# Order of logits, choice and gather in an FFN's token routing, norms on two engines, and output products over all 128 rows

## The chip, the cores and the metric

The kernel runs on one core of a Trainium2 chip. The metric is the time of one execution on the device in microseconds (us). All data are float32, apart from the incidence matrices of layer 1, which the change leaves alone.

## The reference, cut to what matters

Four batches of 128 channels by 64 x 64 tokens (B = 4, C = 128, N = 4096) pass through four layers: a mamba scan (layer 0), a hypergraph convolution with batch norm and SiLU (layer 1), and two blocks of attention and a mixture of experts (layers 2 and 3). Each part of a block works on layer-normed tokens and adds its result to them. The FFN, in short:

```python
# x: layer-normed tokens [B, N, C]; E = 64 experts, K = 8, H = 512
logits = jnp.einsum('bsd,ed->bse', x, gate_w) + gate_b
probs = softmax(logits, axis=1)              # over the tokens
vals, idx = top_k(probs.transpose(0, 2, 1), K)      # 8 tokens for each expert
gathered = ...                               # x at idx: [B, K, E, C]
pooled = jnp.einsum('bked,bke->bed', gathered, vals)
h = gelu(concat(pooled, 1) @ weight1[e], approximate=False)   # per expert
o = concat(h, 1) @ weight2[e]
out = scatter_add(zeros, idx, vals * o)      # back to the 8 tokens of each expert
```

So each expert picks, in each batch, the 8 tokens with the largest softmax over tokens, runs one row through its two matrices, and adds its output to the same 8 tokens with the same weights.

## The kernel before, in words

The residual X lies in SBUF for all of layers 2 and 3: `X[token of tile, batch, tile, channel]`, 32 tiles of 128 tokens a batch. After `layers01()` the order is `layer1_end` (batch norm, SiLU and the turn into X: x loaded on SP, L683, o on ACT, activation L684, POOL's sum L685, TensorE transposes L690, evacuations L692), `attn2`, `ffn("L2_ffn")`, `attn3`, `ffn("L3_ffn", out)`. The functions are written out one after the other. A scheduler then fixes each engine's order of instructions; tile pools give out the buffers, and a pool of a later function lies over tiles of an earlier one where there is room, so that a load or a norm of the next function may be placed early or not, as its buffer is free.

The FFN treats the batches in two pairs p, with two halves r of 64 experts each on the 128 partitions. For each pair:

- Logits. For each of 8 chunks c of 512 tokens and each half r: statistics (`ln_stats`: bn_stats L700 and small instructions, a square root on ScalarE at L711), four norms by VectorE (`normed`, L716) into a tile of `zs` that is kept until the gather, four transposes (L1043), one copy to `zTf` (L1045; ScalarE for r = 0, VectorE for r = 1), one product with the gate's weights (`ps_l`, L1046). After both halves ScalarE adds the bias into `lg` [128 experts of two batches, 4096 tokens] (L1049).
- Choice. MAX8 finds the eight largest of each row (L1053), MATCH_REPLACE8 writes a copy `ch` in which they are replaced by -3e38 (L1055), ScalarE takes Exp of `lg` with its sum (L1059) and Exp of `ch` (L1060), and VectorE subtracts (L1063): zero all over but in the eight chosen places.
- Gather. For each chunk four transposes of `lg` (L1070), a copy `rt` by ScalarE (L1072), and eight products `ps_p` with the kept norms (L1076). The sum is scaled by 1/`den` (L1081), turned (L1083) and written into `pooled` (L1084).

Before, the program text has logits, choice and gather of pair 0, then those of pair 1. After both the experts: 16 groups of 4, each with 2 MB of weights in two loads on SP (L1020, L1023), two buffers deep, and small loads `b1` on ACT (L1025); `ps_h` L1098 and L1100, Gelu L1105, transposes, `ps_eo` L1113. Then the output: `ob` holds each pair's expert outputs with b2 added and the scale `den` (L1132, L1133). In L2 each tile of 512 tokens takes four products of 64 rows, `route[p][rows, cs]` with `obs[p][rows, :]` (L1144), and VectorE adds them to X (L1145). In L3 the output has channels on partitions: four products with the identity turn X (128 rows, L1151), one product of 64 rows and 512 columns adds the experts (L1155), and the tile goes out through an evacuation L1160 (ScalarE for r = 0, VectorE for r = 1) and a DMA on SP. A float32 product runs as two passes on TensorE, so the profile counts two matmuls for each. PSUM holds two buffers each of `ps`, `tr` and `acc`.

`attn3` is untouched, but its rows serve for comparison: it has norms on ScalarE (L905: Identity with scale and bias from pointers), small products L953 and products L965.

Of the kernel before, what the change touches and what calls it, by code (L numbers as in the profile page):

```python
# [19 lines left out]
N = 4096  # L20
CH = 512
NCH = N // CH
NB = N // P
E = 64
HF = 512
TOPK = 8


def bc(ap, n):
# [4 lines left out]
def bc_last(ap, n):  # L34

    return ap.unsqueeze(len(ap.shape)).to_broadcast([*ap.shape, n])


class Net:
# [652 lines left out]
                        (nc.vector.tensor_copy if h else nc.scalar.copy)(self.X[:, b, k : k + 4, :], pt)  # L692


    def ln_stats(self, sp, b, j0, n):
# [6 lines left out]
        rs = sp.tile([P, n], F32, tag="lnrs", name="lnrs")  # L702
# [281 lines left out]
    def ffn(self, name, out=None):  # L984
# [8 lines left out]
        with ExitStack() as ctx:  # L993
# [2 lines left out]
            tp = ctx.enter_context(tc.tile_pool(name="ft", bufs=4))  # L996
            sp = ctx.enter_context(tc.tile_pool(name="fs", bufs=4))
            ew = ctx.enter_context(tc.tile_pool(name="fe", bufs=2))
            ps = ctx.enter_context(tc.tile_pool(name="fps", bufs=2, space=PSUM))
            aps = ctx.enter_context(tc.tile_pool(name="fa", bufs=2, space=PSUM))  # L1000

            gw = wp.tile([E, P], F32, tag="gw", name="gw")
# [14 lines left out]
            def load(g):  # L1017
# [7 lines left out]
                nc.scalar.dma_start(b1, a[f"{name}_weight1"][e0 : e0 + EG, C, :])  # L1025
                return w1, w2, b1

            route, dens = [], []
            for p in range(B // 2):
                lg = big.tile([P, N], F32, tag="lg", name="lg")  # L1030
                zs = [[big.tile([P, 4, P], F32, tag="z", name="zf", bufs=17) for r in range(2)] for c in range(NCH)]
                for c in range(NCH):
                    pl = ps.tile([P, CH], F32, tag="ps", name="ps_l")
                    for r in range(2):
                        if c % 4 == 0:
                            if r == 0:
                                st = {}
                            st[r] = self.ln_stats(sp, 2 * p + r, 4 * c, 16)
                        pt = ps.tile([P, 4, P], F32, tag="tr", name="ps_t")
                        for i in range(4):  # L1040
                            j = 4 * c + i
                            self.normed(zs[c][r][:, i, :], 2 * p + r, j, *st[r], j % 16)
                            nc.tensor.transpose(pt[:, i, :], zs[c][r][:, i, :], self.ident)  # L1043
                        zT = tp.tile([P, 4, P], F32, tag="s", name="zTf")
                        (nc.vector.tensor_copy if r else nc.scalar.copy)(zT, pt)  # L1045
                        nc.tensor.matmul(  # L1046
                            pl[r * E : (r + 1) * E, :], gwT, zT.rearrange("p i c -> p (i c)"), start=True, stop=True
                        )
                    nc.scalar.activation(lg[:, c * CH : (c + 1) * CH], pl, AF.Identity, bias=gb)  # L1049


                m8 = sp.tile([P, TOPK], F32, tag="m8", name="m8")
                nc.vector.max(m8, lg)  # L1053
                ch = wp.tile([P, N], F32, tag="ch", name="ch")
                nc.vector.match_replace(ch, m8, lg, -3.0e38)  # L1055
# [3 lines left out]
                nc.scalar.activation(lg, lg, AF.Exp, bias=nmax, accum_out=den)  # L1059
                nc.scalar.activation(ch, ch, AF.Exp, bias=nmax)  # L1060
                nc.vector.reciprocal(den, den)

                nc.vector.tensor_tensor(lg, lg, ch, ALU.subtract)  # L1063
                route.append(lg)
                dens.append(den)
                pp = aps.tile([P, P], F32, tag="acc", name="ps_p")
                for c in range(NCH):
                    pt = ps.tile([P, 4, P], F32, tag="tr", name="ps_rt")
                    for i in range(4):
                        nc.tensor.transpose(pt[:, i, :], lg[:, (4 * c + i) * P : (4 * c + i + 1) * P], self.ident)  # L1070
                    rt = tp.tile([P, 4, P], F32, tag="s", name="rt")
                    nc.scalar.copy(rt, pt)  # L1072
                    for i in range(4):
                        j = 4 * c + i
                        for r in range(2):
                            nc.tensor.matmul(  # L1076
                                pp[r * E : (r + 1) * E, :], rt[:, i, r * E : (r + 1) * E], zs[c][r][:, i, :],
                                start=j == 0, stop=j == NB - 1,
                            )
# [48 lines left out]
            for p in range(B // 2):  # L1128
                pt = ps.tile([P, P], F32, tag="tr", name="ps_ot")
                nc.tensor.transpose(pt, outT[:, 2 * p : 2 * p + 2, :].rearrange("p b e -> p (b e)"), self.ident)  # L1130
                ob = wp.tile([P, P], F32, tag=f"ob{p}", name="ob")
                nc.vector.tensor_tensor(ob, pt, b2, ALU.add)  # L1132
                nc.vector.tensor_scalar(ob, ob, dens[p], None, ALU.mult)  # L1133
                obs.append(ob)
            for p in range(B // 2):
                for c in range(NCH):
                    for r in range(2):
                        b, rows = 2 * p + r, slice(r * E, (r + 1) * E)
                        x = X[:, b, 4 * c : 4 * c + 4, :]
                        if out is None:  # L1140
                            po = ps.tile([P, 4, P], F32, tag="ps", name="ps_f")
                            for i in range(4):
                                cs = slice((4 * c + i) * P, (4 * c + i + 1) * P)
                                nc.tensor.matmul(po[:, i, :], route[p][rows, cs], obs[p][rows, :], start=True, stop=True)  # L1144
                            nc.vector.tensor_tensor(x, x, po, ALU.add)  # L1145
                        else:

                            sl = slice(c * CH, (c + 1) * CH)
                            po = ps.tile([P, CH], F32, tag="ps", name="ps_f")
                            for i in range(4):  # L1150
                                nc.tensor.matmul(  # L1151
                                    po[:, i * P : (i + 1) * P], x[:, i, :], self.ident,
                                    start=i == 0, stop=False, skip_group_check=True,
                                )
                            nc.tensor.matmul(  # L1155
                                po, obs[p][rows, :], route[p][rows, sl], start=False, stop=True,
                                skip_group_check=True,
                            )
# [65 lines left out]
```

## Time and profile before

| | us |
|---|---|
| three runs | 4468.59, 4474.22, 4481.0 |
| median | 4474.22 |
| the profiled execution | 4388.62 |
| its span | 4386.8, mean granted TensorE clock 0.901 |
| layers 0 and 1 | 0 to 3332 |
| layer1_end | 3334 to 3400 |
| attn2 | 3400 to 3694 |
| FFN of L2 | 3694 to 3948 |
| attn3 | 3948 to 4095 |
| FFN of L3 | 4095 to 4387 |

Inside the FFNs:

| stage | L2 | L3 |
|---|---|---|
| logits, pair 0 | 3694.7 to 3727.7 | 4095.3 to 4125.4 |
| choice, pair 0 | to 3750.2 | to 4147.9 |
| gather, pair 0 | to 3765.5 | to 4165.4 |
| logits, pair 1 | to 3790.2 | to 4188.6 |
| choice, pair 1 | to 3812.5 | to 4210.9 |
| gather, pair 1 | to 3828.0 | to 4226.9 |
| experts | to 3916.9 | to 4316.8 |
| output | to 3947.9 | to 4386 |

The profile is of one execution. PE is TensorE's products, PEld its weight loads, DVE VectorE, ACT ScalarE, POOL GpSimd, SP SyncE, which issues most DMAs. In the views a group or an event is named by engine, line and tile; "<-" names what ended the wait before it. Windows give the busy time of each engine in a stretch, then the granted clock, the DMA's share and GB/s. "issue" is time in which an engine waited for nothing that the profile shows.

### The profile page before, as it was taken

What the parts mean: (1) busy time and instruction counts of PE and PEld (TensorE: products, weight loads), DVE (VectorE), ACT (ScalarE), POOL (GpSimd) and SP (SyncE); (2) the same over time, 40 slices, a digit from 0 to 9 for tenths busy, and PEclk for the clock granted to TensorE, in tenths of its full rate; (3) what the DMA queues carried; (4) which work ended last, traced back from release to release, by engine and by line L of the source; (5) the groups of instructions that cost most, each with busy time, mean ns of one, the idle gap of its engine ahead of it and who ended that gap; (6) DMA issues with size and microseconds to landing.
All of it is one profiled execution on the core that took longest, in us unless ns stands there. A gap on an engine that the chain in (4) does not pass through costs nothing. (4 is left out here: it accounts for less than half of the span.)

```text
span 4386.8 us, 49410 instructions
## 1 busy us (share of the span) xinstructions
PE 3581.4 (82%) x17495; PEld 1997.4 (46%) x17495; DVE 3068.5 (70%) x4945; ACT 2045.6 (47%) x3337; POOL 2465.3 (56%) x1258
## 2 busy tenths in 40 slices
PE   6877758888896888889688888899996899578768
PEld 2333333444543344454334445355653676347534
DVE  5988889997667999766799986744201988428721
ACT  4655654555544445554444556311422564308421
POOL 5999888897787989778788877810003000003100
PEclk8988878899997889999788999999997999799879
DMA  3554545555374445437445553621235000070045
GB/s 104 149 150 147 147 111 134 130 143 135 100 217 113 133 133 139 138 105 210 115 125 136 136 135 104 197 91 63 68 98 204 5 1 2 27 282 3 2 148 199
DMA packets 261737, 524.17 MB, mean 119 GB/s; under 512 B 21962, under 2 KB 24306, under 8 KB 261490
## 3 DMA queue, kind: packets, MB, share of 16 engines
q1 hardware_dynamic: 250194, 501.65, 39.8%
q10 hardware_dynamic: 11296, 19.37, 1.3%
q8 instruction: 138, 2.26, 0.2%
q14 instruction: 109, 0.89, 0.1%
HBM read 443.34 MB, written 77.59 MB: 119 GB/s over the span
## 5 line engine op out<-in xcount | busy, mean ns | idle before, releaser
L284 POOL TENSOR_TENSOR db<-dx,bt 128x1024 f32<-128x1024 f32 x512 | 1203.2, 2354 | 335.0 <-DVE hs L302 219.1
L302 DVE TENSOR_TENSOR_SCAN hs<-hs,carry,db 128x512 f32<-128x512 f32 x812 | 1036.8, 1284 | 173.8 <-ACT hs L296 91.4
L296 ACT ACTIVATE hs<-dl,A 128x512 f32<-128x512 f32 x1024 | 706.6, 692 | 747.5 <-DVE ho L312 693.9
L497 PE MATMUL ps_g<-xn 128*128 128x512 f32 x1152 | 606.4, 657 | 101.3 <-DVE inc L500 77.1
L319 POOL TENSOR_TENSOR ho_s<-ho_s,ho 128x1024 f32<-128x1024 f32 x288 | 677.2, 2351 | 13.7 <-DVE ho L312 13.0
L312 DVE TENSOR_TENSOR ho<-hs,bt 128x1024 f32<-128x1024 f32 x464 | 564.4, 1217 | 1.6
L520 PE MATMUL ps_ed<-xs,inc 128*128 128x258 f16 x4096 | 511.0, 285 | 19.5 <-DVE inc L500 8.8
L520 PEld LDWEIGHTS <-inc 128*128 128x128 fp8e4 x4096 | 416.3, 102 | 134.9 <-issue 62.1
L500 DVE SCALAR_TENSOR_TENSOR inc<-ps_g,hcl,hb 128x512 fp8e4<-128x512 f32 x576 | 421.8, 739 | 39.1 <-PE ps_g L497 23.4
L497 PEld LDWEIGHTS ps_g<-xn 128*128 128x128 f32 x1152 | 216.8, 205 | 420.5 <-DVE inc L500 187.2
L340 PE MATMUL ps_y<-ho,cst 128*128 128x512 f32 x512 | 275.3, 681 | 108.6 <-POOL ho L308 91.4
L620 PE MATMUL ps_v<-inc_v,es 128*128 128x512 fp8e4 x1536 | 342.8, 382 | 20.0 <-DMA bt<-bcd 17.3
L620 PEld LDWEIGHTS <-es 128*128 128x128 f16 x2048 | 202.5, 99 | 289.1 <-issue 63.7
L513 ACT CAST inc<-ps_t 128x512 fp8e4<-128x512 f32 x448 | 232.1, 600 | 95.5 <-PE ps_t L509 95.5
L222 PE MATMUL ps_c<-xt,wc 128*128 128x512 f32 x512 | 234.5, 612 | 10.6 <-DVE inc L500 6.8
L340 PEld LDWEIGHTS ps_y<-ho,cst 128*128 128x128 f32 x512 | 105.5, 215 | 269.7 <-POOL ho L308 121.8
L526 ACT COPY ed<-ps_ed 128x129 f32<-128x129 f32 x128 | 34.0, 266 | 379.7 <-PE ps_ed L520 379.7
L527 DVE TENSOR_TENSOR ed<-ps_ed,ed 128x129 f32<-128x129 f32 x128 | 36.8, 288 | 211.0 <-ACT ed L526 207.9
L302 DVE TENSOR_TENSOR_SCAN hs<-hs,db 128x512 f32<-128x512 f32 x116 | 141.3, 1224 | 53.6 <-POOL db L284 42.6
L536 POOL TENSOR_TENSOR ed<-ed,rdeg 128x512 f32<-128x512 f32 x32 | 33.3, 1039 | 251.1 <-DVE rdeg L532 251.1
L872 POOL MEMSET G<- 128x128 f32 x2 | 0.4, 204 | 300.8 <-PE ps_f L1144 300.8
L222 PEld LDWEIGHTS ps_c<-xt,wc 128*128 128x128 f32 x512 | 99.4, 197 | 136.8 <-issue 116.7
(283 smaller groups left out, 5700.9 us busy)
## 6 DMA issues: line engine op xcount, KB each, us to landing
bt<-bcd SPq DMA_DIRECT2D x512, 512.0 KB
inc<-inc SPq DMA_DIRECT2D x192, 256.0 KB
inc_v<-inc SPq DMA_DIRECT2D x96, 512.0 KB
w<-in_L_ffn_weight SPq DMA_DIRECT2D x32, 1024.0 KB
w2f<-in_L_ffn_weight SPq DMA_DIRECT2D x32, 1024.0 KB
strip<-inc SPq DMA_DIRECT2D x84, 256.0 KB
x<-x ACTq DMA_DIRECT2D x32, 256.0 KB
xn<-x SPq DMA_DIRECT2D x32, 256.0 KB
```

What stands on the lines that cost most here:

```text
L222: nc.tensor.matmul(s["ps"][h], wc[:, h, j, :], xt[:, j : j + T], start=j == 0, stop=j == 3)
L284: nc.gpsimd.tensor_tensor(db, s["dx"], bc(s["bt", n][:, 0, :], 2), ALU.mult)
L296: act(nc.scalar.activation(hs[:, k, :], s["dl"][:, k, :], AF.Exp, scale=A[:, k, n : n + 1]))
L302: nc.vector.tensor_tensor_scan(to[:, h, :], hs[:, h, :], db[:, h, :], init, ALU.mult, ALU.add)
L312: nc.vector.tensor_tensor(ho, hs, ct, ALU.mult)
L319: nc.gpsimd.tensor_tensor(s["sum", n // G], s["sum", n // G], ho, ALU.add)
L340: nc.tensor.matmul(s["y"][h], self.ident, t[:, h, :], start=False, stop=n == DS - 1 and k == len(terms) - 1,)
L497: nc.tensor.matmul(pq, xn[v // 4][:, v % 4 * P : (v % 4 + 1) * P], xn[c], start=True, stop=True)
L500: nc.vector.scalar_tensor_tensor(inc[:, v, :], pq, hc[:, v : v + 1], hb, ALU.subtract, ALU.is_gt, saturate=False)
L513: later(1, lambda: act(nc.scalar.copy(inc[:, v, :], pt, saturate=False)))
L520: nc.tensor.matmul(pe[:, : 2 * P + 2], inc[:, v, i * P : (i + 1) * P], xs[:, v, :], start=v == 0, stop=v == NB - 1,)
L620: nc.tensor.matmul(pv, es[:, e, k, :], inc[:, e, :], start=e == 0 and k == 0, stop=e == NB - 1 and k == 1,)
```

## The change

Four things change, all in `ffn` (and `ln_stats` may write the reciprocal deviations into a tile that it is given):

1. The order of the program text: logits(0), choose(0), logits(1), gather(0), choose(1), gather(1).
2. The norms are not kept. The logits' norms go to tiles of 128 x 128 with 8 buffers; of every four, one is VectorE's and three are ScalarE's (Identity with scale and bias); all `zTf` copies are ScalarE's. The gather multiplies X itself: VectorE multiplies the deviations' reciprocals (`rsk`, kept) into `rt`, and the mean is taken out of the gathered row afterwards, as the mean over its channels.
3. The choice takes one Exp instead of two: `ch` marks the chosen places by TAKEN, and one scalar_tensor_tensor writes Exp where `ch` is TAKEN and zero elsewhere.
4. The expert outputs `ob` are padded with zeros to all 128 rows for each half, so that the output's products take all 128 rows. In L2 one product gives both batches' 256 columns for a tile of 128 tokens. PSUM has three buffers of `ps` and `tr`.

```diff
-            ps = ctx.enter_context(tc.tile_pool(name="fps", bufs=2, space=PSUM))
+            ps = ctx.enter_context(tc.tile_pool(name="fps", bufs=3, space=PSUM))
...
-                zs = [[big.tile([P, 4, P], F32, tag="z", name="zf", bufs=17) for r in range(2)] for c in range(NCH)]
...
+                            z = tp.tile([P, P], F32, tag="z", name="zf", bufs=8)
+                            if i:
+                                k = j % 16
+                                nc.scalar.activation(
+                                    z, X[:, 2 * p + r, j, :], AF.Identity, scale=rs[:, k : k + 1], bias=nb[:, k : k + 1]
+                                )
+                            else:
+                                self.normed(z, 2 * p + r, j, nm, rs, j % 16)
+                            nc.tensor.transpose(pt[:, i, :], z, self.ident)
...
-                        (nc.vector.tensor_copy if r else nc.scalar.copy)(zT, pt)
+                        nc.scalar.copy(zT, pt)
...
-                nc.scalar.activation(ch, ch, AF.Exp, bias=nmax)
...
-                nc.vector.tensor_tensor(lg, lg, ch, ALU.subtract)
+                nc.vector.scalar_tensor_tensor(lg, ch, TAKEN, lg, ALU.is_equal, ALU.mult)
...
-                    nc.scalar.copy(rt, pt)
+                    nc.vector.tensor_tensor(
+                        rt.rearrange("p i (r e) -> p i r e", r=2), pt.rearrange("p i (r e) -> p i r e", r=2),
+                        bc_last(rsk[p][:, 4 * c : 4 * c + 4, :], E), ALU.mult,
+                    )
...
+                m = sp.tile([P, 1], F32, tag="m", name="m")
+                nc.vector.reduce_sum(m, pp, axis=AX.X)
+                nc.vector.tensor_scalar(m, m, -1.0 / C, None, ALU.mult)
...
-                nc.vector.tensor_scalar(pd, pp, den, None, ALU.mult)
+                nc.vector.tensor_scalar(pd, pp, m, dens[p], ALU.add, ALU.mult)
...
+            logits(0)
+            choose(0)
+            logits(1)
+            gather(0)
+            choose(1)
+            gather(1)
...
+                ob = wp.tile([P, 2, P], F32, tag=f"ob{p}", name="ob")
+                nc.gpsimd.memset(ob, 0.0)
+                for r in range(2):
+                    rows = slice(r * E, (r + 1) * E)
+                    nc.vector.tensor_tensor(ob[rows, r, :], pt[rows, :], b2[rows, :], ALU.add)
+                    nc.vector.tensor_scalar(ob[rows, r, :], ob[rows, r, :], dens[p][rows, :], None, ALU.mult)
...
-                                nc.tensor.matmul(po[:, i, :], route[p][rows, cs], obs[p][rows, :], start=True, stop=True)
+                            j = 4 * c + 2 * r
+                            po = ps.tile([P, 2, 2, P], F32, tag="ps", name="ps_f")
+                            for i in range(2):
+                                nc.tensor.matmul(
+                                    po[:, i, :, :].rearrange("p r c -> p (r c)"), route[p][:, (j + i) * P : (j + i + 1) * P],
+                                    obs[p].rearrange("p r c -> p (r c)"), start=True, stop=True,
+                                )
...
-                                po, obs[p][rows, :], route[p][rows, sl], start=False, stop=True,
-                                skip_group_check=True,
+                                po, obs[p][:, r, :], route[p][:, sl], start=False, stop=True, skip_group_check=True
```

More of the change, by code (lines that the diff above doesn't have):

```diff
@@ L26 @@
 TOPK = 8
+TAKEN = -(2.0**127)
 def bc(ap, n):
@@ L692, in layer1_end, with ln_stats @@
                         (nc.vector.tensor_copy if h else nc.scalar.copy)(self.X[:, b, k : k + 4, :], pt)
-    def ln_stats(self, sp, b, j0, n):
+    def ln_stats(self, sp, b, j0, n, rs=None):
         nc, X = self.nc, self.X
@@ L701, in ln_stats @@
         nm = sp.tile([P, n], F32, tag="lnnm", name="lnnm")
-        rs = sp.tile([P, n], F32, tag="lnrs", name="lnrs")
+        if rs is None:
+            rs = sp.tile([P, n], F32, tag="lnrs", name="lnrs")
         d = sp.tile([P, n], F32, tag="lnd", name="lnd")
@@ L1026, in load, with logits @@
                 return w1, w2, b1
+            rsk = [wp.tile([P, NB, 2], F32, tag=f"rs{p}", name="rsk") for p in range(B // 2)]
             route, dens = [], []
-            for p in range(B // 2):
+            def logits(p):
                 lg = big.tile([P, N], F32, tag="lg", name="lg")
-                zs = [[big.tile([P, 4, P], F32, tag="z", name="zf", bufs=17) for r in range(2)] for c in range(NCH)]
+                st = {}
                 for c in range(NCH):
@@ L1035, in ffn @@
                         if c % 4 == 0:
-                            if r == 0:
-                                st = {}
-                            st[r] = self.ln_stats(sp, 2 * p + r, 4 * c, 16)
+                            st[r] = self.ln_stats(sp, 2 * p + r, 4 * c, 16, rsk[p][:, 4 * c : 4 * c + 16, r])
+                            nm, rs = st[r]
+                            nb = sp.tile([P, 16], F32, tag="lnnb", name="lnnb")
+                            nc.vector.tensor_tensor(nb, nm, rs, ALU.mult)
+                            st[r] = nm, rs, nb
+                        nm, rs, nb = st[r]
                         pt = ps.tile([P, 4, P], F32, tag="tr", name="ps_t")
@@ L1041, in ffn @@
                             j = 4 * c + i
-                            self.normed(zs[c][r][:, i, :], 2 * p + r, j, *st[r], j % 16)
-                            nc.tensor.transpose(pt[:, i, :], zs[c][r][:, i, :], self.ident)
+                            z = tp.tile([P, P], F32, tag="z", name="zf", bufs=8)
[7 more added lines that the diff above has]
+                            nc.tensor.transpose(pt[:, i, :], z, self.ident)
                         zT = tp.tile([P, 4, P], F32, tag="s", name="zTf")
-                        (nc.vector.tensor_copy if r else nc.scalar.copy)(zT, pt)
+                        nc.scalar.copy(zT, pt)
                         nc.tensor.matmul(
@@ L1049, in ffn, with choose @@
                     nc.scalar.activation(lg[:, c * CH : (c + 1) * CH], pl, AF.Identity, bias=gb)
+                route.append(lg)
+            def choose(p):
+                lg = route[p]
                 m8 = sp.tile([P, TOPK], F32, tag="m8", name="m8")
@@ L1054, in ffn @@
                 ch = wp.tile([P, N], F32, tag="ch", name="ch")
-                nc.vector.match_replace(ch, m8, lg, -3.0e38)
+                nc.vector.match_replace(ch, m8, lg, TAKEN)
                 nmax = sp.tile([P, 1], F32, tag="nmax", name="nmax")
@@ L1059, in ffn, with gather @@
                 nc.scalar.activation(lg, lg, AF.Exp, bias=nmax, accum_out=den)
-                nc.scalar.activation(ch, ch, AF.Exp, bias=nmax)
+                nc.vector.scalar_tensor_tensor(lg, ch, TAKEN, lg, ALU.is_equal, ALU.mult)
                 nc.vector.reciprocal(den, den)
-                nc.vector.tensor_tensor(lg, lg, ch, ALU.subtract)
-                route.append(lg)
                 dens.append(den)
+            def gather(p):
+                lg = route[p]
                 pp = aps.tile([P, P], F32, tag="acc", name="ps_p")
@@ L1076, in ffn @@
                             nc.tensor.matmul(
-                                pp[r * E : (r + 1) * E, :], rt[:, i, r * E : (r + 1) * E], zs[c][r][:, i, :],
+                                pp[r * E : (r + 1) * E, :], rt[:, i, r * E : (r + 1) * E], X[:, 2 * p + r, j, :],
                                 start=j == 0, stop=j == NB - 1,
                             )
+                m = sp.tile([P, 1], F32, tag="m", name="m")
+                nc.vector.reduce_sum(m, pp, axis=AX.X)
+                nc.vector.tensor_scalar(m, m, -1.0 / C, None, ALU.mult)
                 pd = tp.tile([P, P], F32, tag="s2", name="pd", bufs=3)
-                nc.vector.tensor_scalar(pd, pp, den, None, ALU.mult)
+                nc.vector.tensor_scalar(pd, pp, m, dens[p], ALU.add, ALU.mult)
                 pt = ps.tile([P, P], F32, tag="tr", name="ps_pt")
@@ L1130, in ffn @@
                 nc.tensor.transpose(pt, outT[:, 2 * p : 2 * p + 2, :].rearrange("p b e -> p (b e)"), self.ident)
-                ob = wp.tile([P, P], F32, tag=f"ob{p}", name="ob")
-                nc.vector.tensor_tensor(ob, pt, b2, ALU.add)
-                nc.vector.tensor_scalar(ob, ob, dens[p], None, ALU.mult)
+                ob = wp.tile([P, 2, P], F32, tag=f"ob{p}", name="ob")
[4 more added lines that the diff above has]
+                    nc.vector.tensor_scalar(ob[rows, r, :], ob[rows, r, :], dens[p][rows, :], None, ALU.mult)
                 obs.append(ob)
@@ L1137, in ffn @@
                     for r in range(2):
-                        b, rows = 2 * p + r, slice(r * E, (r + 1) * E)
-                        x = X[:, b, 4 * c : 4 * c + 4, :]
                         if out is None:
-                            po = ps.tile([P, 4, P], F32, tag="ps", name="ps_f")
-                            for i in range(4):
-                                cs = slice((4 * c + i) * P, (4 * c + i + 1) * P)
-                                nc.tensor.matmul(po[:, i, :], route[p][rows, cs], obs[p][rows, :], start=True, stop=True)
+                            j = 4 * c + 2 * r
[5 more added lines that the diff above has]
+                                )
+                            x = X[:, 2 * p : 2 * p + 2, j : j + 2, :].rearrange("p r i c -> p i r c")
                             nc.vector.tensor_tensor(x, x, po, ALU.add)
                         else:
+                            b = 2 * p + r
                             sl = slice(c * CH, (c + 1) * CH)
@@ L1151, in ffn @@
                                 nc.tensor.matmul(
-                                    po[:, i * P : (i + 1) * P], x[:, i, :], self.ident,
+                                    po[:, i * P : (i + 1) * P], X[:, b, 4 * c + i, :], self.ident,
                                     start=i == 0, stop=False, skip_group_check=True,
```

## The prediction

> **What bounds the kernel now.** Layers 0 and 1 (0 to 3332 us) are the same instructions in both kernels, so I read only what follows, and in it the two FFN layers (L2 at 3694 to 3948, L3 at 4095 to 4387). First the chain of waits inside the first FFN: who is late in the choice of tokens.
>
> ```profile
> 3727.70 4.43 DVE m L1053
> 3732.38 4.40 DVE ch L1055 x2
> 3736.91 1.28 ACT L1059
> 3738.21 3.80 ACT lg L1059 x2
> 3742.01 3.61 ACT ch L1060
> 3745.64 4.44 DVE lg L1063
> 3750.21 1.94 PE ps_rt L1070 x8
> ```
>
> The choice is one serial line of whole-row instructions, 22.5 us from MAX8 to the first gather transpose, and it comes twice per layer with TensorE waiting. The windows view gives each stage's engines (PE, PEld, DVE, ACT, POOL busy, then granted clock, DMA share, GB/s).
>
> ```profile
> 3340.00:3400.00 60.00, 31.12 (x128) 24.73 (x126) 11.05 (x17) 24.78 (x29) 34.79 (x21) 0.50 0.78 276
> 3728.00:3750.00 22.00, 0.00 (x0) 0.00 (x0) 14.46 (x16) 10.33 (x7) 0.00 (x0) 0.56 0.00 0
> 3766.00:3790.00 24.00, 21.78 (x97) 9.79 (x94) 9.74 (x25) 9.66 (x16) 0.00 (x0) 1.00 0.00 0
> 3828.00:3914.00 86.00, 66.68 (x744) 31.52 (x744) 11.89 (x19) 12.48 (x20) 0.00 (x0) 0.90 0.93 344
> 4317.00:4386.00 69.00, 65.20 (x304) 37.94 (x302) 11.07 (x16) 9.36 (x16) 0.00 (x0) 1.00 0.33 122
> ```
>
> TensorE stands still through the choice (0.00 of 22). The second pair's logits (3766 to 3790) are TensorE's: 21.78 of 24 us, 2.88 per chunk of 512 tokens. The experts (3828 to 3914) are bound by their weights, DMA share 0.93 at 344 GB/s. L3's output (4317 to 4386) is TensorE's, with the DMA only a third busy. The groups of instructions by line, 3695 to 3790, price the logits:
>
> ```profile
> L716 DVE TENSOR_SCALAR zf<-X,lnnm,lnrs 128x128 f32<-128x128 f32 x125 | 33.4, 343 | 3.9 <-PE ps_p L1076 3.9
> L1049 ACT ACTIVATE lg<-ps_l,gb 128x512 f32<-128x512 f32 x16 | 11.0, 687 | 28.6 <-PE ps_l L1046 28.6
> L1045 ACT COPY zTf<-ps_t 128x512 f32<-128x512 f32 x16 | 9.3, 583 | 12.7 <-PE ps_t L1043 6.6 <-DVE gwT L70 6.1
> ```
>
> and attn3 already holds the ScalarE norm that the change will use (scale and bias from pointers):
>
> ```profile
> L905 ACT ACTIVATE z<-X,lnnb,lnrs 128x128 f32<-128x128 f32 x7 | 3.4, 492 | 0.1
> ```
>
> Last, L3's output in the timeline, PE and then its weight loads:
>
> ```profile
> 4341.13 1.12 PE L1155 MATMUL ps_f<-lg,ob 64*128 64x512 f32 x2
> 4342.18 1.16 PE L1151 MATMUL ps_f<-cst,X 128*128 128x128 f32 x8
> 4343.27 1.12 PE L1155 MATMUL ps_f<-lg,ob 64*128 64x512 f32 x2
> 4342.18 0.97 PEld L1151 LDWEIGHTS ps_f<-cst,X 128*128 128x128 f32 x8 [0.76 <-issue]
> ```
>
> One tile of 512 tokens takes 2.14 us (4341.13 to 4343.27). In each tile PE goes from products of 64 rows to products of 128 rows and back, and the weight loads stand 0.76 us for nothing the profile shows.
>
> **The sum's base.** The durations are of the profiled execution: 4388.62 us, 4386.8 of it span. The median of the timed runs is 4474.22, 85.6 us (2%) above it; I carry that difference over unchanged.
>
> **L3 output, 128 rows instead of 64.** The products stay the same in number and columns; the added rows multiply zeros. At the spacing of unbroken passes in other stages (0.107 us for 128 columns, 0.427 for 512) a tile is 8 x 0.107 + 2 x 0.427 = 1.71 us. Row minus this: 0.43 x 32 tiles = -13.7. Bounds: 0 if the stand has another cause than the change of row count, -13.7 if it goes whole. I take -13.7, since attn3 passes from L953 to L965, both 128 rows, at 0.53 us between starts with no such stand. What is late next: 8.4 MB of output in 55 us are 153 GB/s, where the expert stage drew 344; evacuations are 0.69 per two tiles on each of DVE and ACT. [...]
>
> **L2 output.** 256 passes of 128 columns become 128 of 256: the same 27.3 us of PE. Now two tiles take 3.87 us and hold a stand of 0.18 to 0.23 us each for DVE's X with two PSUM buffers (31.0 us in all); a third buffer takes it away: -3.5 (bounds 0 and -3.7). DVE's 0.60 a tile (19 us) stays below PE. ob's four half-row pairs instead of two cost +0.2 to +0.9 once; taken in this.
>
> **What the front holds.** Of each pair's 64 norms, 48 go to ACT, and all 16 zT copies. ACT per chunk, back to back: 6 x 0.40 (an L905 starts at 4063.30, ACT's next work at 4063.70) + 2 x 0.485 + 0.59 = 3.96 us against PE's 2.88. ACT becomes the bound: 31.7 us a pair. In the changed program as built, ACT's order is copy, one norm, lg, so lg waits for the ps_l of the copy just made: copy to lg is 1.73 us in this trace, and one norm covers 0.40. Worked by hand this comes to 4.87 us a chunk, 39 a pair. [...]
>
> First MAX8 (T0), L2: before 3727.7. After, the norms start at about 3701.0 (before, the first zT copy was at 3697.9), since all 128 bn_stats of both pairs (26 us of DVE) now stand in this logits stage: the built order has none of them in attn2's tail. With 31.7 us and 5 of fill T0 is 3737.8 (+10), with stalls 3744 (+16). L3: before 4125.4; after 4132 (+7) to 4138 (+13).
>
> From T0 to the second MAX8 (T1), before: choice 22.5, gather 15.3, logits 24.6, 62.5 in all (63.2 in L3). After, gather(0) stands behind logits(1) on PE, and runs in the second choice, where PE was idle. But the Exp of choose(0) stands in ACT's queue behind the first tile only of logits(1), and ACT runs in order: it is held for MAX8 4.43, MATCH_REPLACE8 4.41, small work, table load 1.28 and Exp 3.9, together 14.4 us; all norms, copies and lg behind it wait, and PE with them. DVE's product of 4.43 then holds up its own norms for some 1.5. What is left, 45 norms, 15 copies, 8 lg, is 30 us without stalls and 37 with. T1 = T0 + 46 to 52. So T1 moves by -6.5 to +6 in L2 and by -10 to +2 in L3. The stalls are in the built order, so I take +5 and +1.
>
> After T1: the second Exp (3.69) and the table load (1.28) go, six rt copies of gather(0) at 0.62 enter DVE's queue between the steps (+3.7), the mean's reduce and scale add 0.6: -1 a layer (bounds 0 and -2.3). Gelu's table load (1.28, on the path at 3829.21, behind ps_h) now waits only for DVE and can come early: -1.3 a layer.
>
> **layer1_end.** The dropped zf tiles (34 KB a partition) move the buffers. Before, L2's first 4 MB of expert weights are issued on SP from 3334.7, among the x loads of layer1_end; the POOL timeline shows it:
>
> ```profile
> 3348.05 2.34 POOL L685 TENSOR_TENSOR x<-x,o 128x1024 f32<-128x1024 f32 x1 [3.86 <-DMA x<-x]
> 3381.48 4.64 POOL L685 TENSOR_TENSOR x<-x,o 128x1024 f32<-128x1024 f32 x2 [3.06 <-ACT o L684]
> ```
>
> After, these loads stand behind the x loads and wait for attn2's tiles. Pairs of tiles took 9.0, 8.4 and 8.4 us early and 7.7 later: 1.3 + 0.7 + 0.7 + some 2.5 at the start = -5 (bounds 0, -6). They then load during logits(0), which moves 0 GB/s now, and are needed only in the expert stage. Two small b1 loads move with them, on ACT's queue, from layer1_end to just ahead of gw's load and the first norm; at SP's 0.38 us an issue (the row of 3829.16) 0.8 us, inside the spread of T0.
>
> **Sum:** -5 + 5 + 1 - 2 - 2.6 - 3.5 - 13.7 = -20.8, so 4367.8 profiled and about 4453 at the median.
>
> **Rivals.** (1) No stalls: ACT runs back to back, fronts at -6.5 and -10, so -37.3, or 4437. For it: three PSUM buffers and eight z tiles. Against: lg's place in ACT's queue. (2) Slower: PE's clock. In ACT-bound logits PE has 2.57 us of full-speed work in 4.87 us a chunk. layer1_end, half busy, was granted 0.50 (window above). If logits get that, ps_l's 0.87 a chunk doubles behind lg: 0.87 x 8 x 4 = +28; if the transposes' 0.85 a chunk show too, +55. Total +7 to +34, middle 4494; it decides from about two fifths of the logits' time at half clock. Against: 3900 to 3910, PE busy 6.84 of 10, was granted 1.00. (3) The switch of rows is not what stands in L3's output: the sum without its 13.7 is -7, or 4467, within 0.3% (13.4 us, about what a measurement of this kernel can tell from no change). (4) The early weight loads cost layer1_end nothing: -16, inside the forecast's spread.
>
> **How the numbers follow.** Forecast with (4) 0.47, rival 1 0.18, rival 2 0.15, rival 3 0.20. Range: 4429 (rival 1 with the other terms at their ends, -45) to 4490 (rival 2 in its lower half, +16). Faster: rival 1 and most of the forecast, 0.60; same: rival 3 and the forecast's weak edge, 0.25; slower: rival 2, 0.15.
>
> **What would show it.** L3's output tiles at 1.71 and no "issue" stand in PEld; two L2 tiles at about 3.4; ACT above 80% busy in both logits stages, with waits on ps_l at lg; T1 - T0 near 50; PE at work under the second MAX8; POOL in layer1_end without the 3.86 wait. I am wrong if L3's tiles stay at 2.14, if the logits' clock falls under 0.8, or if expert stages lengthen past 86 and 89 us.

## The result and the profile after

The median after is 4421.43 us (20 runs, 4407.76 to 4434.39) against 4431.99 for before (20 runs, 4397.44 to 4481.0); the ratio of the comparison is 0.9996, 95% interval 0.9978 to 1.0014. Ratios, here and below, leave out runs over 1.5% above their kernel's fastest (seven of before's 20; the other 13 have a median of 4423.1). So the change made no difference that can be measured. The forecast was 4453, faster. Note the two spreads: 27 us after, 84 us before. The three runs of before that the forecast had were all from the upper part of its spread, and its profiled execution (4388.62) was faster than all 20 runs.

The profiled execution of after has a span of 4427.4 us, 40.6 us more than that of before. Stage by stage, from the starts and ends in the timelines (the first row from the first POOL sum of layer1_end, the last to the span's end; T0 and T1 are the MAX8 starts of the two pairs):

| stage | before | after | difference |
|---|---|---|---|
| layer1_end | 62.8 | 62.0 | -0.8 |
| attn2 | 294.6 | 306.2 | +11.6 |
| L2: to T0 | 33.1 | 54.7 | +21.6 |
| L2: T0 to T1 | 62.5 | 57.7 | -4.8 |
| L2: choice 1, gather 1 | 37.9 | 36.3 | -1.6 |
| L2: experts | 88.9 | 101.4 | +12.5 |
| L2: output | 31.5 | 30.4 | -1.1 |
| attn3 | 146.9 | 146.2 | -0.7 |
| L3: to T0 | 30.1 | 44.1 | +14.0 |
| L3: T0 to T1 | 63.2 | 56.1 | -7.1 |
| L3: choice 1, gather 1 | 38.3 | 37.1 | -1.2 |
| L3: experts | 89.8 | 101.3 | +11.5 |
| L3: output | 70.0 | 57.5 | -12.5 |

The chain of waits of L2's choice, after:

```profile
3759.15 4.43 DVE m L1072
3763.71 4.40 DVE ch L1074
3768.26 1.27 ACT L1078
3769.54 3.80 ACT lg L1078 x2
...
3833.25 4.42 DVE lg L1080
3837.82 1.94 PE ps_rt L1092 x8
```

The second Exp is gone, and MAX8 starts 31.5 us later than before. The windows view, with the columns as in the prediction:

```profile
3705.00:3760.00 55.00, 33.74 (x101) 11.93 (x101) 35.60 (x201) 37.24 (x84) 0.23 (x1) 0.84 0.22 78
3772.00:3815.00 43.00, 31.87 (x97) 11.58 (x97) 10.53 (x18) 31.80 (x69) 0.00 (x0) 0.86 0.00 0
3853.00:3954.00 101.00, 80.96 (x748) 38.16 (x748) 12.95 (x24) 11.89 (x20) 0.00 (x0) 0.70 0.85 299
4372.00:4427.00 55.00, 51.58 (x292) 36.94 (x290) 11.06 (x16) 8.78 (x15) 0.00 (x0) 0.99 0.41 153
```

First logits, second logits, experts, L3's output. In the second logits ScalarE is as busy as TensorE (31.80 and 31.87 of 43). The experts, whose instructions are unchanged, got a clock of 0.70 and 299 GB/s; before it was 0.90 and 344. ScalarE's groups in L3's first logits (4130 to 4175), and the first of its waits there:

```profile
L1053 ACT ACTIVATE zf<-X,lnnb,rsk 128x128 f32<-128x128 f32 x49 | 21.0, 488 | 0.0
L1060 ACT COPY zTf<-ps_t 128x512 f32<-128x512 f32 x16 | 9.3, 583 | 2.0 <-PE ps_t L1058 1.6
```

```profile
ACT lg L1064 <- PE ps_l L1061: 6.2, 8, 0.8
```

21.0 us of norms and 0.8 of waiting at each of eight lg: the cycle that was worked out by hand is there. Two chunks take 9.90 us (lg at 4140.28 and 4150.18), where 9.74 was foretold. L3's output, PE and then its weight loads:

```profile
4396.28 1.02 PE L1198 MATMUL ps_f<-lg,ob 128*128 128x512 f32 x2
4397.14 1.05 PE L1194 MATMUL ps_f<-cst,X 128*128 128x128 f32 x8
4395.39 0.86 PEld L1194 LDWEIGHTS ps_f<-cst,X 128*128 128x128 f32 x7 [0.24 <-issue]
```

The period is 1.75 us (4394.53, 4396.28, 4398.03) in place of 2.14. The weight loads have two stands of 0.24 a tile, one before a single load and one before the other seven, in place of one of 0.76. In layer1_end the chunk that had waited 3.86 us for x waits 3.06 for ScalarE now, so that only 0.8 us of that wait is gone:

```profile
3346.28 2.34 POOL L686 TENSOR_TENSOR x<-x,o 128x1024 f32<-128x1024 f32 x1 [3.06 <-ACT o L685]
```

### The profile page after: what moved, and what is told of

Same layout as the page of the kernel before. It is cut to its first block, busy times and chain, and to the rows that moved or that the text cites. A ratio compares the mean times of both kernels' runs of the same rounds, so it can differ in the third digit from the quotient of the medians.

```text
span 4427.4 us, 49138 instructions
## 1 busy us (share of the span) xinstructions
PE 3637.5 (82%) x17367; PEld 2017.9 (46%) x17367; DVE 3026.8 (68%) x4785; ACT 2093.8 (47%) x3515; POOL 2465.8 (56%) x1262
## 5 line engine op out<-in xcount | busy, mean ns | idle before, releaser
L320 POOL TENSOR_TENSOR ho_s<-ho_s,ho 128x1024 f32<-128x1024 f32 x288 | 677.6, 2353 | 16.8 <-DVE ho L313 16.1
L510 PE MATMUL ps_t<-ident,strip 128*128 128x128 fp8e4 x1344 | 114.9, 227 | 53.4 <-DVE ed L528 18.6
```

Source lines behind the costliest of these rows:

```text
L320: nc.gpsimd.tensor_tensor(s["sum", n // G], s["sum", n // G], ho, ALU.add)
```

## The experiments

All were timed in five rounds against the kernel before on the same chip. Theory A: at an equal clock the change loses some 17 us, by the moved buffers (attn2, gw) and by ScalarE in the logits, while the granted clock (the share of TensorE's full clock that the profile shows as granted), in stages that the forecast took as fixed, moves the whole time by as much. Its main rivals: the layout is harmless and the norms cost it all; the clock differs in all stages alike; the output's gain is lost behind it. At first A had the clock in the expert stages only.

**The kernel before, once more**, unchanged.

> The kernel before, unchanged, for a second profile of it. Theory A (the expert stage has two paces, and which one an execution gets is chance): the profile before had its 16 groups of L2 at 5.4 us each, at a granted clock of 0.90, and an execution at the other pace needs 7.46 us a group, as 4320 to 4368 of the profile after shows; so this profile may show an expert stage of up to 119 us in place of 86, at a clock near 0.6, and nothing else moved by over 3 us. Rival B (the 85 us between the first profile and the median lie in layers 0 and 1, or in all stages evenly): the expert stages keep 86 to 89 us, and another stage differs.

Measured: 4463.75 (12 runs, 4402.65 to 4488.7), ratio 0.9989 (0.9947 to 1.003), as it should be. Theory A as put there was half right. The expert stage of L2 took 103.3 us, L3's 89.6; but most of the extra time lies elsewhere, in the outputs: 46.1 us in L2 (before 31.5) and 126.5 in L3 (before 70.0). The windows of those two, and PE in the second:

```profile
3920.70:3966.70 46.00, 45.32 (x256) 44.70 (x256) 22.06 (x34) 0.00 (x0) 0.57 (x5) 0.51 0.22 83
4333.80:4460.30 126.50, 121.89 (x304) 68.65 (x304) 11.25 (x17) 9.36 (x16) 0.00 (x0) 0.50 0.18 67
```

```profile
4388.26 2.07 PE L1151 MATMUL ps_f<-cst,X 128*128 128x128 f32 x8
4390.27 2.07 PE L1155 MATMUL ps_f<-lg,ob 64*128 64x512 f32 x2
```

The same instructions were granted 1.00 in the first profile and 0.50 here, with PE busy 121.89 of 126.50 us; a tile takes 4.0 us. The 12 runs fall in two groups, five up to 4425.57 and seven from 4462.13, 37 us apart. In the clock records of before's and after's traces the granted clock is 0.5 or 1.0 in each of 220 stretches, and each lasts a multiple of 3.41 us (the last stretch is cut off). An engine busy for 96% of 126 us kept the half clock here: being busy was not enough. In both stages the clock was 1.00 up to the output (windows 3911.2 to 3920.7 and 4290 to 4333.8), and 0.51 and 0.50 over the output's whole length.

**After, with the dropped tiles' room kept**

```diff
+            room = big.tile([P, 7168], F32, tag="room", name="room", bufs=1)
+            nc.gpsimd.memset(room[:, :4], 0.0)
             rsk = [wp.tile([P, NB, 2], F32, tag=f"rs{p}", name="rsk") for p in range(B // 2)]
```

> The kernel after, with 28 KB a partition kept as an empty tile in the pool where the dropped zf tiles lay, so that the FFN's buffers lie where they lay before. Theory A (the change of layout cost attn2 and the start of the FFN): attn2's steps go from 9.24 us back to 8.36 (-12 us in all), gw lands ahead of the first norm in L2 (-4), statistics return to attn2's tail, layer1_end +1: -15, near 4406 at after's median of 4421. Rival B (the norms on ScalarE cost the time, the layout nothing): attn2's steps stay at 9.24 or the time stays within 5 us of after.

Measured: 4401.48, ratio 0.9945 (0.9918 to 0.9973), and 20 us below after's median (of another comparison). attn2 takes 291.2 us in place of 306.2, L2's way to T0 48.8 in place of 54.7. What had happened to attn2, which nobody touched, shows in ScalarE's timeline of one step, first before, then after:

```profile
3632.59 1.07 ACT L778 COPY qkT<-ps_qkT 128x512 f32<-128x512 f32 x2 [2.22 <-PE ps_qkT L775]
3633.55 1.08 ACT L763 ACTIVATE ex<-qkv 128x1024 f32<-128x1024 f32 x1
```

```profile
3627.43 0.58 ACT L780 COPY qkT<-ps_qkT 128x512 f32<-128x512 f32 x1 [2.22 <-PE ps_qkT L777]
3627.91 1.06 ACT L765 ACTIVATE ex<-qkv 128x1024 f32<-128x1024 f32 x1
3628.88 0.58 ACT L780 COPY qkT<-ps_qkT 128x512 f32<-128x512 f32 x1
```

Before, both copies of qkT run ahead of the activation. After, the scheduler puts the activation between them, the second copy is 0.97 us later, PE waits for it (0.29 at ps_a, where it had run on), and twelve of the 32 steps take 9.24 us in place of 8.36, although VectorE has no statistics of the FFN in it any more. With the room kept the copies are together again and the step is 8.36 (copies at 3611.76, 3620.13, 3628.49). The other part of the 20 us is L2's way to T0. The gate's weights gw were issued behind the first loads of the moved expert weights and landed after 6.24 us, with the FFN's first instructions behind them:

```profile
3704.56 6.24 DMA gw<-in_L_ffn_gate_w
```

Their transpose starts 6.5 us after the issue, with the room kept 2.1. That is 4.4 of the 5.9 us. The rest isn't separated: 125 bn_stats stand in this stretch after, 64 with the room kept.

**Before, with only the output changed** (padded ob, products of 128 rows, three PSUM buffers):

```diff
...
-                            nc.tensor.matmul(
-                                po, obs[p][rows, :], route[p][rows, sl], start=False, stop=True,
+                            nc.tensor.matmul(
+                                po, obs[p][:, r, :], route[p][:, sl], start=False, stop=True, skip_group_check=True
```

> The kernel before with only the output's part of the change: padded ob, products of 128 rows, three PSUM buffers of ps and tr. Theory A: L3's output at 1.75 us a tile in place of 2.14 (-12.5), L2's output -1 to -3.5, nothing else: -14 to -16, ratio 0.9965 to before. Rival B (the gain in the output is lost elsewhere in the chain, for example because DMA of the output or the next attention is late): the output's tiles shorten and the end does not come earlier by over 5 us.

Measured: 4385.33 (7 runs, 4380.39 to 4397.2), ratio 0.9911 (0.9878 to 0.9943): more than twice what was expected. L3's output takes 57.5 us, as expected, at full clock; the spread of before is gone. And the logits got shorter: T0 after 30.4 and 28.3 us, T0 to T1 57.6 and 57.9. The output's gain and the steadiness are read as the rows' doing, the shorter logits are tested by the next run. L2's output, with its 128 rows, was entered at 0.50, and the clock was 1.00 again 3.5 us later (in after 3.8 us), where the outputs of 64 rows in before_again had 0.51 over 46.0 us and 0.50 over 126.5:

```profile
3932.70:3936.20 3.50, 3.49 (x8) 2.85 (x9) 1.73 (x5) 0.00 (x0) 0.00 (x0) 0.51 1.05 370
3936.20:3963.00 26.80, 26.08 (x121) 22.61 (x119) 21.30 (x33) 0.00 (x0) 0.52 (x4) 1.00 0.20 76
```

**Before, with three PSUM buffers and nothing else**

```diff
-            ps = ctx.enter_context(tc.tile_pool(name="fps", bufs=2, space=PSUM))
+            ps = ctx.enter_context(tc.tile_pool(name="fps", bufs=3, space=PSUM))
```

> The kernel before with three PSUM buffers of ps and tr in place of two, nothing else; outputs of 64 rows. Theory A (the third buffer, not the output, shortened the logits in before_outputs): T0 at 30.4 and 28.3 us after the attentions in place of 33.1 and 30.1, T0 to T1 57.7 in place of 62.5 and 63.2, about -14 us in the profile outside the output stages; L3's output still 70 us or 126 by its clock, so the runs still spread over 50 us or more. Rival B (the shorter logits came with the output's other tiles): logits as in before.

Measured: 4390.08 (12 runs), ratio 0.992 (0.9884 to 0.9957). T0 after 30.8 and 28.3, T0 to T1 58.7 and 58.3: -12.8 us over the four stages. So the old logits were not at TensorE's limit: the 2.88 us a chunk, 2.38 on average in the second pair with the third buffer, are read as the latency of a chain through two buffers. The runs lie in two groups still, nine from 4368.31 to 4394.05 and three from 4426.64 to 4448.34: the third buffer shortens, the rows steady (16.8 us from the lowest to the highest run in before_outputs, 80.0 here). In this profile a tile of L3's output still takes 2.14 us, so the 1.75 is the rows' doing. But L2's output, with its 64 rows, takes 23.3 us, where 128 rows take 28.6 at the full clock:

```profile
3920.50:3943.80 23.30, 22.53 (x256) 22.34 (x256) 20.38 (x35) 0.00 (x0) 0.66 (x5) 0.92 0.42 154
```

It was entered at half clock and got the full one back after 3.7 us. So an output of 64 rows doesn't always stay at half clock, and in L2 the padding costs 5.3 us once there are three buffers. The expert stages took 101.9 and 101.7 us, 13 and 12 more than before, with no change but the buffer.

**After, with more work for TensorE in the experts**

```diff
                     ph = ps.tile([P, HF], F32, tag="ps", name="ps_h")
+                    nc.tensor.matmul(
+                        ph, self.ident, X[:, 0, 0:4, :].rearrange("p i c -> p (i c)"), start=True, stop=True,
+                        skip_group_check=True,
+                    )
```

> The kernel after with one more product in each group of experts: 128 rows, 512 columns, X against the identity, into the buffer of ps_h ahead of the products that clear it; its result is not used. It adds 0.85 us of TensorE work to each of the 32 groups at full clock. Theory A (the granted clock follows the work done per time; a group at half clock does too little of it to get the full clock back, and stays at 7.46 us): with the added work the stage is granted the full clock nearly throughout, a group takes 5.3 to 5.6 us (DMA), the two stages fall from 101 and 100 us to 86 to 92: -20 us or more. Rival B (the clock has another cause, or TensorE's own work is the bound): the stages get longer, by 0.85 to 1.7 us a group, +27 to +54 us.

Measured: 4399.45 (11 runs, 4391.26 to 4402.65), ratio 0.9937 (0.9912 to 0.9962), 22 us below after's median (of another comparison). The stages are 89.3 and 88.8 us long; windows of the two:

```profile
3843.60:3932.90 89.30, 70.69 (x774) 32.19 (x774) 13.36 (x25) 11.89 (x20) 0.00 (x0) 1.00 0.94 338
4243.20:4332.00 88.80, 73.17 (x798) 35.11 (x799) 13.12 (x24) 11.89 (x20) 0.00 (x0) 1.00 0.93 333
```

32 more products, and each stage 12 us shorter: the clock is 1.00 throughout, where after had 0.70 in L2's, and the weights' DMA, with shares of 0.94 and 0.93, is the bound again. So more work did not lower the clock in the experts, it came with a higher one. Whether the amount of work counts or the length of the gaps, which the product fills too, this run can't tell.

**Before, with that product** and its old outputs.

> The kernel before, outputs of 64 rows as they were, with the added product in each group of experts. Both expert stages then end at full clock (88 to 90 us). [...] Rival B (the outputs only inherited a half clock from the expert stages): outputs of 31.5 and 70 us in each execution, runs within 20 us of each other, near 4372.

Measured: 4397.6 (12 runs, 4378.39 to 4458.16), ratio 0.991 (0.9865 to 0.9955); nine runs up to 4403.64, three from 4438.57. The experts are at 1.00, and the two outputs of this one execution are:

```profile
3920.70:3965.90 45.20, 44.29 (x256) 43.52 (x256) 21.98 (x34) 0.00 (x0) 0.57 (x5) 0.53 0.23 86
4331.80:4401.80 70.00, 65.42 (x304) 38.17 (x304) 11.21 (x17) 9.38 (x16) 0.00 (x0) 0.99 0.32 120
```

L2's was entered at the full clock of the experts (1.00 from 3917 to 3921) and had 0.53 over its length, 0.50 from 3924.4 to 3931.2, so some 3 us at the full one ((0.53 - 0.50) / 0.50 of 45.2); L3's kept it. So the outputs of 64 rows don't inherit the half clock from the experts; they can fall to it by themselves. With 128 rows L3's output took 57.5 to 59.2 us in all ten profiles that have them.

**The choice of tokens alone.** With the busy experts and outputs of 128 rows on both sides, and the room kept on after's, the two fronts can be compared at an equal clock.

> The kernel before with the new output (before_outputs) and the added product in each group of experts (as after_busy). Theory A (before_outputs holds its expert stages of 115 and 104 us by a half clock): both expert stages 89 us at clock 1.00, the time near 4385 - 25 = 4360, the runs within 15 us of each other. Rival B (the front of before leaves the experts in another state than that of after): the stages stay above 95 us.

Measured: 4357.29 (6 runs), ratio 0.9865 (0.9839 to 0.9892), experts 89.3 and 88.2.

> The kernel after with the room kept (after_room) and the added product (after_busy): all that differs from before_outputs_busy is then the choice of tokens. Theory A (the two fronts lose, stage by stage: L2 +15.7 to T0, -5.4 to T1, L3 +14.1 and -7.2, -2.6 behind it; attn2 -3): +12 us to before_outputs_busy, near 4372. Rival B (the fronts' loss was the clock's): within 4 us of before_outputs_busy.

Measured: 4380.06 (6 runs), ratio 0.9919 (0.9889 to 0.9948): 22.8 us behind the other, where 12 were expected. T0 comes 17.8 us (L2) and 15.8 us (L3) later, T0 to T1 is 1.5 and 1.9 us shorter, the rest -1.9 and -2.3, attn2 -2.5. The miss is the third PSUM buffer, whose gain in the old logits I had not seen when I wrote the expectation. So once both have that buffer, the reordered front with ScalarE's norms saves next to nothing between T0 and T1 and loses 34 us ahead of T0.

**The order undone** (room_busy with gather(0) ahead of logits(1)):

> room_busy with the program order of before (logits, choice and gather of pair 0, then pair 1): what the new order alone is worth. Theory A (the order gains what gather(0) took, 15.4 us, and the first tile's work, less the rt copies it puts into the second choice): from T0 to T1 21 + 15.4 + 39 = 75 in place of 56 us, and the second choice 3.7 us shorter: +15 a layer, +30 us to room_busy, near 4410. Rival B (with ScalarE held by the first Exp the order hides nothing): under +10 us.

Measured: 4410.36, ratio 0.9943 (0.9909 to 0.9977), 30 us more than room_busy (in another comparison; both to before). T0 to T1 73.2 and 72.4, the second choice 17.4. With three of four norms on ScalarE the order by itself is good for 17 us a layer between T0 and T1, less 3.6 in the second choice. Its worth with other norms is not shown.

**Half of the norms on ScalarE, or none.** One line of room_busy each (`if i % 2:`; and no norm on ScalarE with the zTf copies shared as before).

> room_busy with two of four norms on ScalarE in place of three. Theory A (ScalarE is the bound of the logits, 4.9 us a chunk with its waits at lg): two norms fewer a chunk take 0.8 us from it, in 8 chunks of the first pair and 7 of the second, in two layers: -20 us if the waits at lg stay as they are, -12 if they grow. Rival B (the in-order queue, not ScalarE's load, sets the pace): under 6 us.

> room_busy with all norms on VectorE and the zTf copies shared as before (ScalarE r = 0, VectorE r = 1): the new order, one Exp and the gather from X alone. Theory A: L2's and L3's first logits return to 30 to 34 us (-14 each); from T0 to T1 the second pair's norms stand behind VectorE's choice (13.3 us of whole-row work), so about 50 to 57 us are left; -28 to room_busy, or -16 to before_outputs_busy. Rival B (VectorE, with 26 us of bn_stats, becomes the bound): T0 no earlier than in room_busy.

Measured: half 4356.08, ratio 0.9864 (0.9838 to 0.9889), none 4354.3, ratio 0.9859 (0.9832 to 0.9885): 24 and 26 us below room_busy. With none, T0 is after 34.0 and 30.6 us, as expected; T0 to T1 55.5 and 56.5. With half, 40.6 and 37.9, then 50.2 and 50.4. The two end at nearly the same T1, 90 us after attn2 in L2, by different ways. Both are within 3 us of before_outputs_busy (4357.29, the same comparison), which has before's front. So with three buffers and the full clock on both sides, the new order, the single Exp and the gather from X together are worth nothing that these runs can tell, where the expectation had -16.

**The two better halves together** (first pair as in "none", second as in "half"):

> The two better halves put together: the first pair's norms all on VectorE with zTf copies shared, as in room_busy_dve, the second pair's norms half on ScalarE with its copies, as in room_busy_half. Theory A (each stage keeps its own length: T0 after 34 and 30.6 us, T0 to T1 50.3, the second choice 21.0): -7 us a layer to room_busy_half, near 4342 and -2.1% to before. Rival B (the scheduler moves the second pair's statistics or the stages share a bound): within 4 us of room_busy_half.

Measured: 4351.92 (6 runs, 4347.6 to 4361.02), ratio 0.9812 (0.9761 to 0.9863), the lowest median of all, but only 4 us below room_busy_half, and in another comparison: rival B. T0 comes early (34.0, 30.6), but T0 to T1 is 56.3 and 54.0. Windows of L3 from T0 on, first of the mix, then of half:

```profile
4117.80:4135.00 17.20, 0.00 (x0) 0.00 (x0) 17.19 (x41) 6.87 (x6) 0.00 (x0) 0.54 0.00 0
```

```profile
4120.40:4138.00 17.60, 8.07 (x16) 2.40 (x16) 13.16 (x9) 10.58 (x15) 0.00 (x0) 0.62 0.00 0
```

In the mix the second pair's statistics fill VectorE between the steps of the choice (17.19 of 17.20 us, 41 instructions against 9), and TensorE has nothing; in half they were done while T0 was waited for, and TensorE did 8.07 us of the next logits. What is gained ahead of T0 is paid back behind it.

## Why the prediction was wrong

- **The sum's base** is the step that failed first. "The median of the timed runs is 4474.22, 85.6 us (2%) above it; I carry that difference over unchanged." The difference was no constant: a second profile of before, 73.5 us longer than the first, has 56.5 more in L3's output and 14.6 in L2's, the stages whose instructions the change replaces, and 14.4 in L2's experts. The three runs shown were of the upper group (before's 20-run median is 4431.99), and after's runs have no such group. That is also why 4421.43 fell below the low end of 4429. The sign of the sum failed by itself, in attn2 and in the way to T1 (below).
- **L3 output**: right in size at equal clock, -12.5 for -13.7, and the rows are the cause that was named; 2.1 of the stage came with the third buffer alone. Whether the change of row count costs the time, or the 64 rows themselves, no run separates. What I left out is worth more in many executions: at half clock the same stage takes 126.5 us, and with 128 rows it had a clock of 0.96 to 1.00 in all ten profiles. I had PE's clock among the rivals, but asked only whether the logits would lose it.
- **L2 output**: -1.1 in this pair of profiles, -2.9 in the eight later ones with 28.6 us, for -3.5. The buffer alone gave -8.2 (before_psum), so that "the same 27.3 us of PE" was no bound for 64 rows, and the padding gave part of it back.
- **layer1_end**: -0.8 for -5. The early weight loads, which after_room brings back, cost 62.8 against 62.0. The wait of 3.86 gave 0.8, since the next wait took its place. The first pair's 9.0 us stayed (9.03). The two pairs of 8.4 fell to 7.7, as foretold, but the last sums came 1.25 us later in turn.
- **attn2**: +11.6 for 0. I read the built order for the FFN's instructions and missed that attn2's own had changed. after_room takes the 11.6 away with an empty tile.
- **T0 and T1**: the hand-worked cycle of 4.87 us is measured at 4.95, and ScalarE as the bound is shown (24 us back with a third of its norms moved to VectorE). I put T1 at +5 and +1; it was +16.8 and +6.9. Of L2's miss 5.9 us come from the layout, most of them by gw's load behind the moved weights, a wait that the sum did not have. The 2.88 us a chunk that I read as TensorE's bound were none: before_psum took the old logits below it, to 2.38 us on average in the second pair.
- **Behind T1**: -1.6 and -1.2 for -2.3 a layer (-1 and -1.3 for Gelu's table).
- **Experts**: expected unchanged, +12.5 and +11.5 in this pair of profiles. This was one of the prediction's own signs of being wrong, and what holds the clock down there is open. Without the added product, before's two profiles, with two PSUM buffers, have one long stage of four (103.3; 88.9, 89.8 and 89.6), so chance plays a part. The four kernels with three buffers (before_psum, before_outputs, after, after_room) have eight of eight, 96.5 to 114.7. The third buffer, which the change brings, may be the cause, since before_psum differs from before in nothing else; with chance in play its one profile doesn't prove it.

At equal clock this adds up to +17.6 us for after (the table's 40.6 + 1.0 from an earlier start of layer1_end, less 24.0 in the experts), where the sum said -20.8. If the third buffer slows the experts, the 24.0 are the change's own too. The median's zero is read as that loss against the half-clock outputs that it no longer has. The split of the two profiles is shown stage by stage, the balance in the runs is not. Before's median lies 43 us above its first profile, and no profile of a run near it was taken; an output of L2 and an expert stage as in before_again would make 29 of the 43 (an estimate from its 14.6 and 14.4). How often before's outputs are at half clock is known only from the groups of its runs (7 of 12, and 3 of 12 in two variants), so the +17.6 cannot be turned into 0 to the microsecond.

Of the rivals, (3) had the right verdict, within 0.3%, for a wrong reason, and so by luck; L3's tiles did get shorter. (2), the clock, weighed most, but not in the logits, which had 0.84 and 0.92 to T0: in the outputs, to the change's advantage, and in the experts, against it. (1) was added up wrongly: -6.5 and -10 in place of +5 and +1 make -43.3, or 4431, not -37.3.

## What to carry to other kernels

When the profiled execution and the timed runs differ by more than an edit is worth, find the stage that holds the difference before pricing the edit: profile the unchanged kernel again and compare the granted clock stage by stage. Compare the built order of every stage that shares memory with the edited one, not only of the edited one; freed memory alone moved 20 us here. And test "this engine is the bound" before building on it: a third PSUM buffer alone gave 12.8 us in the logits, and with it the new front had nothing left to gain; a third of ScalarE's norms moved back gave 24.

## What the runs showed of the hardware that I had not expected

- An output of 64-row products, in L3 in turn with 128-row ones, can run at a granted clock of 0.50 for 126 us with TensorE busy 96%, and at 1.00 in another execution of the same program (before, 4317 to 4386). With 128 rows throughout it had 0.96 to 1.00 in ten profiles, and where L2's was entered at 0.50 it had 1.00 after 3.5 and 3.8 us.
- The expert stage (products of 32 columns, a wait for weights in each group) has two paces, some 5.4 us a group over the 86 us of before's L2, at a clock of 0.90, and 7.46 in after's L3 from 4321.60 to 4329.07, at 0.50. One more full product a group kept the clock at 1.00 in all eight profiles that had it, and cut 12 us from each stage of after.
- With 128 rows in place of 64 in one product of five, a tile of L3's output takes 1.75 us in place of 2.14, with three PSUM buffers on both sides. What the 0.39 us are made of is not shown.
- With two PSUM buffers L2's output of 64 rows took 1.75 us for 16 passes and then stood 0.18; with three (before_psum), 41 passes took 3.40 us, which is 0.083 a pass in place of 0.109, and the stage 23.3 us in place of 31.5.
